# Two-layer perceiver on one core: the turned context rows of the second cross attention kept in DRAM and loaded, with deeper buffers, all norms of the samples at once, and a unit's exponential one step later

## The chip, the cores and the metric

The kernel runs on one core of one Trainium2 chip. The metric is the time of one execution on the device in microseconds (us), as the median of several runs. Besides the times there is one profiled execution of the kernel: a trace of every instruction on TensorE (PE, with its weight loads apart as PEld), VectorE (DVE), ScalarE (ACT), GpSimd (POOL) and SyncE (SP), of the DMA queues, and of the clock that TensorE was granted (1.00 is full speed).

## The reference

Sixteen samples `x` of 64 rows by 256 attend to sixteen contexts `ctx` of 1601 rows by 256. Two layers follow each other, all in float32. In each, a cross attention, a second mixing layer and a layer of experts are added to `x` in turn, each on the normalised `x`.

```
# layer 0, cross attention: 16 heads of 16, 5 sample points a head
K, V = ctx @ Wk.T + bk, ctx @ Wv.T + bv             # all 1601 rows
Qp = norm(x) @ Wq.T + bq;  off = Qp @ Woff.T + boff
ix = (position + off) mod length, scaled             # a real number per point
sk, sv = 0.5*((1-f)*K[floor(ix)] + f*K[floor(ix)+1]), the same with V
x += (softmax_over_5(Qp . sk / sqrt(16)) . sv) @ Wo.T + bo
# layer 0: sigmoid self attention, then 8 gelu experts, the best 2 of each row
# layer 1, cross attention: 16 heads of 64 over the same context
text, image = ctx[:, :77], ctx[:, 77:]               # 77 and 1524 rows
y  = softmax(q . (text Wk).T / 8) . (text Wv)
y += softmax(q . (image Wk_ip).T / 8) . (image Wv_ip)
x += y @ Wo.T + bo
# layer 1: state space scan over 64 rows, then 32 experts (best 4) and a shared one
```

The context is read twice: layer 0 projects all rows to keys and values, layer 1 uses the 77 text rows and the 1524 image rows of the same array.

## The kernel before

**Keys and values of layer 0.** `spans` (L237) cuts the 1601 rows of each sample into three stretches of 512 and a last one of 65. A stretch of 512 lies in a tile `cx` with four neighbouring rows on each of 128 partitions; `cx_load` (L240) loads it on SP's DMA queue, two stretches ahead, into two buffers. `keys_values` (L369) runs seven steps a sample: TensorE turns two rows a partition (four transposes of 128x128 at L153), ScalarE copies the result into `cxt` (L398), and TensorE multiplies the stretch before, already turned, by the joined key and value weights `wkv` (four banks of 128x512 in PSUM, L381 through L88). ScalarE copies each bank into the tile `kv` (L382, two buffers), and when a stretch is whole, ScalarE's DMA queue writes it to a table `tab` in DRAM (L385), one table for two samples.

**Sample points.** Beside these steps runs the generator `samples` (L300), four groups of two tiles of 128 rows. Each group normalises its rows (`normed`: VectorE's statistics and ScalarE's square root at L99), turns them, projects them to queries and offsets, and computes the indices `ix` and weights `wt` in some forty VectorE instructions. One step of it is issued with each step of the keys and values.

**Text rows.** From step 18 on the generator `texts` (L485) projects the 77 text rows of each sample to the keys and values of layer 1. Keys go to `ktd` in DRAM, kept sample by sample, in four stores for each four pairs of heads (L524); values go to `vtd`.

**Gathers and units.** From step 14 on, GpSimd gathers the sampled key and value rows out of the tables: `gather` (L416) issues ten indirect DMAs (L429), two of which halves make a unit of four heads for 128 rows; there are 32 units. `attend` (L436) works on a unit in two steps: the first forms the scores on VectorE and ends with the exponential on ScalarE (L459), the second normalises (L461 on) and weighs the values. `tick` (L1511) decides when: it is called between pieces of TensorE work with an estimate of their time in us, opens a new half unit every 16 of these us (12 in the cross attention), and takes the next step of a unit 42 after its gathers. `attended` counts finished units; it decides when the middle layers (self attention, experts) may use a tile and how long the plain cross steps run.

**Cross attention of layer 1.** The class `Cross` (L907) takes one sample and one pair of heads a step, 128 steps and three more to run out. The image rows of a sample lie in `cn` as they are in DRAM (`loads`, L915: eleven rows on each partition and 116 rows over, two buffers) with a column of ones added. For the scores they are needed turned: `turn` (L937) does that once a sample, 24 transposes on TensorE and ten copies, shared by VectorE (L84) and ScalarE, into `cT`, of which there is one buffer. It is called in the last step of the sample before (L1102), and for sample 0 in `begin` (L1175). A step (`step`, L1070) issues on TensorE: the scores of twelve blocks of 128 rows in three banks (L1087), the turn and the output of the step before the last (`turn_out`, L1061; `out`, L1020), the first third of the product of the step before with `cn` (`product`, L1059), the transposes that form the row maximum (L1109, L1119), the second third, the queries of the next step folded through the key weights (`fold`, L1015), the last third. VectorE takes the maxima straight from the banks (L1090), subtracts the maximum `mc` into `pt` (L1130), and ScalarE takes the exponentials there (L1131). The 116 rows over go by themselves (L1133, L1134), so there are four subtractions and four exponentials a step. In the middle of the step and at its end generators of other work are advanced by a step: first the rest of layer 0, then the state space (`Ssm`) and the router of layer 1.

**Order.** The instructions of TensorE, VectorE and ScalarE run in the order in which the program issues them (L1527). SP's and GpSimd's are ordered by the framework's scheduler, so a load is issued as soon as its buffer is free and those queued ahead of it are out. Each engine and each queue is in order: an instruction that waits holds what stands behind it.

**Memory on the chip.** `qbds` (queries in blocks) and `pts` (exponentials) are taken at the start from the pool `xw` (L217, L219) and zeroed by GpSimd (L1528 to L1531), though the cross attention alone uses them. The pool `kvp` of the keys and values is closed at the end of that stage, before `Cross` takes `cn` and `cT`.

Of the kernel before, what the change touches and what calls it, by code (L numbers as in the profile page):

```python
# [37 lines left out]
CM = IMG // P  # L38
CR = IMG - CM * P
NCH = CM + 1  # L40
NB = NCH // 4

# [23 lines left out]
def perceiver_kernel(ctx: ExitStack, tc: tile.TileContext, a: dict, out: bass.AP):  # L66
# [150 lines left out]
    qbds = [mk(xw, [P, NHP, 2, 2, S], f"qbd{i}") for i in range(2)]  # L217

    pts = [mk(xw, [P, NCH, P], f"pt{i}") for i in range(2)]  # L219
    tables = [mk(dram, [H0 * M, 4 * HD0], f"tab{j}") for j in range(NPAIR)]  # L220
    ktd = mk(dram, [B, P, NHP, TEXT], "ktd")
# [15 lines left out]
    spans = [(b, m0, RP if M - m0 >= RP * P else 1) for b in range(B) for m0 in range(0, M, RP * P)]  # L237
    cxs = {}

    def cx_load(i):  # L240
        if i < len(spans):
            b, m0, r = spans[i]
            w = min(P, M - m0)
            cx = cxs[i] = mk(kvp, [P, RP, D], "cx", bufs=2)
            nc.sync.dma_start(
                out=cx[:w, :r, :], in_=a["ctx"][b, m0 : m0 + w * r, :].rearrange("(p r) d -> p r d", r=r)
            )
# [3 lines left out]
    cx_load(1)  # L251
    nc.scalar.dma_start(out=x4, in_=a["x"].rearrange("(t p) d -> p t d", p=P))
# [46 lines left out]

    def samples(g):  # L300

        t0 = g * TG
        xn = normed(range(t0, t0 + TG), "s", sp)
        for _ in range(4 if g else 2):
            yield
        xt = turned(xn, TG, "s", sp)
        yield
# [9 lines left out]
        yield  # L317
# [3 lines left out]
        for t in range(TG):  # L321
# [13 lines left out]
            nc.vector.tensor_scalar(xs, xs, sgn[:, c], 1.0 / (M - 1), ALU.mult, ALU.mult)  # L335
        nc.vector.tensor_scalar(x_, x_, 2.0, -1.0, ALU.mult, ALU.add)
# [8 lines left out]
        nc.vector.tensor_tensor(x_, x_, f0, ALU.subtract)  # L345
        wg_ = wt[:, t0 : t0 + TG]
# [6 lines left out]
        for t in range(TG):  # L353
            j = t0 + t
            nc.vector.tensor_scalar(wt[:, j], wt[:, j], zl[:, j : j + 1], None, ALU.add)
            nc.vector.tensor_tensor(f0[:, t, :], f0[:, t, :], hbase, ALU.add)

# [9 lines left out]
        yield  # L367

    def keys_values():  # L369
# [3 lines left out]
        def project(i, cxt, q):  # L373
            nonlocal kv
            b, m0, r = spans[i]
            w = min(P, M - m0)
            if q == 0:
                kv = mk(kvp, [P, H0, RP, 2 * HD0], "kv", bufs=2)
# [11 lines left out]
        for i, (b, m0, r) in enumerate(spans):  # L390
            w = min(P, M - m0)
            cx = cxs.pop(i)
            cxt = mk(kvp, [P, RP, KC, P], "cxt")
            steps = (r + 1) // 2
            for q in range(steps):
# [4 lines left out]
                )  # L400
                if q + 1 == steps:
                    cx_load(i + 2)
# [33 lines left out]
    def attend(i):  # L436
# [21 lines left out]
        nc.vector.tensor_tensor(sc, sc, mx.unsqueeze(2).to_broadcast([P, HU, NK]), ALU.subtract)  # L458
        nc.scalar.activation(sc, sc, AF.Exp, scale=0.5 / math.sqrt(HD0))  # L459
# [1283 lines left out]
```

## Time and profile before

| | |
|---|---|
| median of 5 runs | 3315.1 us (3302.52 to 3331.89) |
| the profiled execution | 3343.09 us, span 3341.1 us |
| mean granted clock | 0.941 |
| TensorE busy | 2934.0 us, 88% of the span |
| VectorE, ScalarE, GpSimd busy | 1620.2, 1026.0, 819.1 us |
| moved by DMA | 326.06 MB, 97 GB/s over the span |

The span falls into stages that differ in what they wait for:

| from to (us) | work |
|---|---|
| 0 to 727 | keys and values of layer 0, sample points, text rows, first gathers, part of the middle layers |
| 727 to 942 | the rest of the middle layers, with gathers |
| 942 to 1400 | first steps of the cross attention, with the last gathers |
| 1400 to 1850 | cross attention beside the rest of layer 0 |
| 1850 to 3045 | cross attention beside the state space |
| 3045 to 3341 | the last experts |

In the profile a group such as "L88 PE MATMUL st<-qf,cT" is a line, an engine, an operation, the tile written and the tiles read; `st` and `mm` are banks of PSUM. A wait names the engine and the line that ended it; "remote" is a wait whose releaser the trace does not show. A share of DMA is the mean busy share of the core's 16 DMA engines. The chain of waits is followed back from the last instruction of the execution.

### The profile page before, as it was taken

To read this page: it belongs to the slowest core of one execution; us is meant where nothing else is said; L and a number is where in the kernel's file an instruction comes from. 1 tells how busy PE (TensorE), PEld (TensorE's weight loads), DVE (VectorE), ACT (ScalarE), POOL (GpSimd) and SP (SyncE) were. 2 spreads that over 40 slices of the span, in tenths; PEclk is the share of its full clock that TensorE was granted. 3 is DMA by queue.
4 is the path that set the end of the run, shared out by engine and by line. 5 is a ranking of instruction groups with operands and counts; after the bars stand their busy time and mean duration, and the time that the engine had idled before them with its cause. 6 is when DMAs were issued, how large, how long until landed. Compare 5 with 4: busy or idle time off the path is not lost.

```text
span 3341.1 us, 46546 instructions
## 1 busy us (share of the span) xinstructions
PE 2934.0 (88%) x17734; PEld 2405.1 (72%) x17734; DVE 1620.2 (48%) x4143; ACT 1026.0 (31%) x2379; POOL 819.1 (25%) x923
## 2 busy tenths in 40 slices
PE   8779877995668788888899899999999999999879
PEld 4444433564567777777798899989999999896667
DVE  2421113223345454555432567557754477655846
ACT  3223333432211221233243333334323343222421
POOL 0444334545535455300001001001100011000721
PEclk9889988997779898898999999999999999999999
DMA  6387754572421112111355212112210122003884
GB/s 201 101 142 153 244 154 110 166 205 80 126 63 31 45 42 60 44 49 34 101 174 167 61 55 65 49 43 69 68 34 30 43 73 65 29 1 105 254 244 123
DMA packets 339015, 326.06 MB, mean 98 GB/s; under 512 B 59349, under 2 KB 289017, under 8 KB 338281
## 3 DMA queue, kind: packets, MB, share of 16 engines
q1 hardware_dynamic: 186297, 225.11, 22.7%
q10 hardware_dynamic: 126928, 63.06, 6.8%
q0 software_dynamic: 25568, 34.91, 5.0%
q8 instruction: 141, 2.31, 0.3%
q14 instruction: 81, 0.66, 0.1%
HBM read 248.37 MB, written 74.62 MB: 97 GB/s over the span
## 4 chain that ended last, share of the span: by engine, by line
PE 75%; DVE 11%; another core or an unknown queue 5%; issue 3%; ACT 3%; DMA 3%; POOL 0%; SPq 0%; DVEq 0%; ACTq 0%; POOLq 0%
PE st L88 31%; PE mm L1059 19%; PE mm L88 16%; PE mm L153 5%; PE mm L1015 2%; DVE hs L1298 1%; PE mm L1045 1%; DVE mp L1090 1%; PE mm L984 1%; DMA wg<-in_guT 1%; DVE pt L1130 1%; PE mm L1109 1%; DVE hc L1303 0%; DMA yk<-y0d,sli 0%
## 5 line engine op out<-in xcount | busy, mean ns | idle before, releaser
L429 POOL DMA_INDIRECT g<-tab,ig x640 | 617.0, 964 | 751.4 <-DVE ig L427 548.8
L88 PE MATMUL st<-qf,cT 128*128 128x128 f32 x6144 | 761.8, 282 | 37.5 <-issue 19.9
L88 PEld LDWEIGHTS st<-qf,cT 128*128 128x128 f32 x6144 | 741.4, 199 | 46.1 <-issue 22.3
L1059 PE MATMUL mm<-cn,pt 128*128 128x257 f32 (+1 forms) x3072 | 757.0, 390 | 4.3 <-DVE cT L84 2.1
L1059 PEld LDWEIGHTS mm<-cn,pt 128*128 128x128 f32 (+1 forms) x3072 | 564.6, 193 | 92.1 <-issue 4.1
L88 PE MATMUL st<-wkv,cxt 128*128 128x512 f32 (+1 forms) x832 | 407.7, 637 | 54.0 <-ACT kv L382 34.6
L1090 DVE TENSOR_REDUCE mp<-st 128x128 f32<-128x512 f32 x384 | 261.1, 688 | 251.7 <-PE st L88 228.5
L88 PEld LDWEIGHTS st<-wkv,cxt 128*128 128x128 f32 (+1 forms) x832 | 159.7, 201 | 230.9 <-issue 174.6
L1130 DVE TENSOR_TENSOR pt<-st,mc 128x512 f32<-128x512 f32 (+1 forms) x384 | 224.2, 639 | 151.9 <-ACT mc L1121 141.4
L1131 ACT ACTIVATE pt<-pt 128x512 f32<-128x512 f32 (+1 forms) x384 | 207.1, 588 | 58.1 <-DVE pt L1130 53.2
L382 ACT COPY kv<-st 128x512 f32<-128x512 f32 (+1 forms) x208 | 119.4, 591 | 240.7 <-PE st L88 136.6
L1121 ACT COPY mc<-mm 128x128 f32<-128x128 f32 x128 | 33.9, 265 | 460.1 <-PE mm L1119 343.6
L1111 DVE TENSOR_REDUCE xmx<-mm 128x1 f32<-128x128 f32 x128 | 37.3, 292 | 231.2 <-PE mm L1109 180.4
L1068 ACT COPY ot<-mm 128x256 f32<-128x256 f32 x128 | 47.2, 369 | 300.0 <-PE mm L153 299.9
L920 POOL MEMSET cn<- 128x12 f32 x16 | 1.8, 120 | 549.5 <-PE mm L1059 519.1
L461 DVE TENSOR_REDUCE smx<-sc 128x4 f32<-128x20 f32 x32 | 5.4, 168 | 250.3 <-ACT sc L459 250.0
L1304 POOL TENSOR_TENSOR ys<-ys,hc 128x512 f32<-128x512 f32 x64 | 81.5, 1274 | 161.2 <-DVE hc L1303 160.9
L88 PE MATMUL mm<-xt,w 128*128 128x256 f32 (+1 forms) x512 | 102.8, 355 | 19.5 <-issue 11.6
L1388 POOL DMA_INDIRECT xb<-xnd,row x55 | 55.3, 1006 | 261.9 <-PE mm L1045 221.6
L88 PEld LDWEIGHTS mm<-xt,w 128*128 128x128 f32 x512 | 88.1, 214 | 37.7 <-issue 23.8
L1035 ACT COPY yt<-mm 128x64 f32<-128x64 f32 x128 | 27.1, 212 | 253.4 <-PE mm L88 219.9
L398 ACT COPY cxt<-mm 128x512 f32<-128x512 f32 (+1 forms) x112 | 60.8, 543 | 99.8 <-PE st L88 31.0
(455 smaller groups left out, 3986.9 us busy)
## 6 DMA issues: line engine op xcount, KB each, us to landing
tab<-kv ACTq DMA_DIRECT2D x48, 1024.0 KB
w<-in_gate SPq DMA_DIRECT2D x66, 512.0 KB
cx<-in_ctx SPq DMA_DIRECT2D x48, 512.0 KB
cn<-in_ctx SPq DMA_DIRECT2D x16, 1408.0 KB
wg<-in_guT SPq DMA_DIRECT2D x87, 256.0 KB
w<-in_lin SPq DMA_DIRECT2D x33, 512.0 KB
wk<-in_xwkiT SPq DMA_DIRECT2D x32, 512.0 KB
wd<-in_down1T SPq DMA_DIRECT2D x87, 128.0 KB
```

Source lines behind the costliest of these rows:

```text
L88: nc.tensor.matmul(o, lhsT=l, rhs=r, start=i == 0, stop=i == len(pairs) - 1)
L153: nc.tensor.transpose(t[:ncol, i, :rows], b, ident[:rows, :rows])
L382: nc.scalar.copy(kv[:w, :, c, :], pk[:w].rearrange("p (h e) -> p h e", h=H0))
L398: nc.scalar.copy(cxt[:, 2 * q : 2 * q + m, :, :w].rearrange("p r k n -> p (r k) n"), tp[:, : KC * m, :w])
L429: nc.gpsimd.indirect_dma_start(out=gf[:, (half * n + s) * 4 * HD0 : (half * n + s + 1) * 4 * HD0], out_offset=None, in_=tables[j], in_offs ...
L1015: nc.tensor.matmul(pf[:, k * P : (k + 1) * P], lhsT=w[:, hp % 4, k * P : (k + 1) * P], rhs=rhs, start=True, stop=True)
L1059: nc.tensor.matmul(po, lhsT=pt[:w, c, :], rhs=cn[:w, c, :], start=c == 0, stop=c == NCH - 1)
L1090: nc.vector.tensor_reduce(mp_[:, i, :], s.rearrange("p c n -> p n c"), AX.X, ALU.max)
L1130: nc.vector.tensor_tensor(o, st[i][:, :m, :], mc.to_broadcast([P, m, P]), ALU.subtract)
L1131: nc.scalar.activation(o, o, AF.Exp)
L1304: nc.gpsimd.tensor_tensor(y, y, hc, ALU.add)
L1388: nc.gpsimd.indirect_dma_start(out=x, out_offset=None, in_=xnd, in_offset=bass.IndirectOffsetOnAxis(ap=tb.row[:, i : i + 1], axis=0))
```

## The change

Image rows are cut as 512, 512 and 500, behind the 77 text rows, so that the stretches that layer 0 turns are those that the cross attention scores; what lies in `cxt` after a stretch is turned is stored to a new array `ctd` in DRAM, 512 KB a stretch, on SP's queue, and `turn` becomes three loads of 512 KB. The scores read these three tiles, `product` takes 128, 128 or 125 partitions a block, and three full subtractions and exponentials replace three and the one for the rest. The 125 wide stretch has its last three columns filled by two small copies (16 samples, two a sample). `turn(0)` moves from `begin` to just behind `loads(0)`, ahead of the middle layers.

More buffers ahead: `cx` three instead of two (a stretch is loaded three ahead), `cxt` three instead of two, `kv` four instead of two. To have the memory, `qbds` and `pts` are taken from a pool opened after the keys and values, and zeroed there (the zeroing of `pts` goes), and two tiles of the state space share the buffers of others.

The samples' rows are normalised and turned in one piece for all eight tiles; the groups take slices of it, and their work is spread over more steps. A unit takes three steps instead of two: a step ends ahead of the exponential, which is issued with the next. Text keys are stored for four samples side by side, one store instead of four.

```diff
-CM = IMG // P
-CR = IMG - CM * P
-NCH = CM + 1
-NB = NCH // 4
+SPAN = (P, P, 125)
+NB = len(SPAN)
+NCH = NB * RP
...
-    qbds = [mk(xw, [P, NHP, 2, 2, S], f"qbd{i}") for i in range(2)]
-
-    pts = [mk(xw, [P, NCH, P], f"pt{i}") for i in range(2)]
+    qbds = []
+
+    pts = []
...
-    ktd = mk(dram, [B, P, NHP, TEXT], "ktd")
+    ktd = mk(dram, [B // 4, P, NHP, 4 * TEXT], "ktd")
...
-    spans = [(b, m0, RP if M - m0 >= RP * P else 1) for b in range(B) for m0 in range(0, M, RP * P)]
+    spans = [(b, m0, w, r) for b in range(B) for m0, w, r in [(0, TEXT, 1)] + [(TEXT + s * RP * P, w, RP) for s, w in enumerate(SPAN)]]
+
+    ctd = mk(dram, [B, NB, P, RP * KC * P], "ctd")
...
-            cx = cxs[i] = mk(kvp, [P, RP, D], "cx", bufs=2)
+            cx = cxs[i] = mk(kvp, [P, RP, D], "cx", bufs=3)
...
     cx_load(1)
+    cx_load(2)
...
+    def turn_all():
+
+        xn = normed(range(NPAIR), "s", sp)
+        for _ in range(3):
+            yield
+        xts.append(turned(xn, NPAIR, "s", sp))
+        yield
+
+    xts = []
+
     def samples(g):
 
+
         t0 = g * TG
-        xn = normed(range(t0, t0 + TG), "s", sp)
-        for _ in range(4 if g else 2):
-            yield
-        xt = turned(xn, TG, "s", sp)
-        yield
+        xt = xts[0][:, :, g * TOK : (g + 1) * TOK]
+
+        def rest():
+            yield
+            if g:
+                yield
+
...
-        yield
+        yield from rest()
...
             if q == 0:
-                kv = mk(kvp, [P, H0, RP, 2 * HD0], "kv", bufs=2)
+                kv = mk(kvp, [P, H0, RP, 2 * HD0], "kv", bufs=4)
...
-            cxt = mk(kvp, [P, RP, KC, P], "cxt")
+            cxt = mk(kvp, [P, RP, KC, P], "cxt", bufs=3)
...
+                if r > 1 and w < P:
+
+                    nc.scalar.copy(
+                        cxt[:, 2 * q : 2 * q + m, :, w:].rearrange("p r k n -> p (r k) n"), tp[:, : KC * m, : P - w]
+                    )
                 if q + 1 == steps:
-                    cx_load(i + 2)
+                    cx_load(i + 3)
+                    if r > 1:
+                        nc.sync.dma_start(out=ctd[b, (m0 - TEXT) // (RP * P)], in_=cxt.rearrange("p r k n -> p (r k n)"))
...
         nc.vector.tensor_tensor(sc, sc, mx.unsqueeze(2).to_broadcast([P, HU, NK]), ALU.subtract)
+        yield
         nc.scalar.activation(sc, sc, AF.Exp, scale=0.5 / math.sqrt(HD0))
...
                 if hp % 4 == 3:
-                    for i in range(4):
-                        nc.sync.dma_start(out=ktd[q * 4 + i, :, hp - 3 : hp + 1, :], in_=kt[:, :, i * TEXT : (i + 1) * TEXT])
+                    nc.sync.dma_start(out=ktd[q, :, hp - 3 : hp + 1, :], in_=kt)
...
-            nc.sync.dma_start(
-                out=cn[:, :CM, :D], in_=a["ctx"][b, TEXT : TEXT + CM * P, :].rearrange("(p c) d -> p c d", c=CM)
-            )
-            nc.sync.dma_start(out=cn[:CR, CM, :D], in_=a["ctx"][b, TEXT + CM * P :, :])
+            m0 = TEXT
+            for i, w in enumerate(SPAN):
+                nc.sync.dma_start(
+                    out=cn[:w, i * RP : (i + 1) * RP, :D], in_=a["ctx"][b, m0 : m0 + w * RP, :].rearrange("(p r) d -> p r d", r=RP)
+                )
+                m0 += w * RP
...
-            self.kt[b] = load(self.xp, "kt", ktd[b], [P, NHP, TEXT], 1)
+            self.kt[b] = load(self.xp, "kt", ktd[b // 4, :, :, b % 4 * TEXT : (b % 4 + 1) * TEXT], [P, NHP, TEXT], 1)
...
-            cn = self.cn[b]
-            ct = self.ctx[b] = mk(self.xc, [P, KC, NCH * P], "cT", bufs=1)
-            i = 0
-            for k in range(KC):
-                d = slice(k * P, (k + 1) * P)
-                for c in range(0, CM, 4):
...
+            self.ctx[b] = [
+                load(self.xc, f"ct{i}", ctd[b, i].rearrange("p (r k n) -> p r k n", r=RP, k=KC), [P, RP, KC, P], 1) for i in range(NB)
+            ]
...
-                w = P if c < CM else CR
+                w = SPAN[c // RP]
...
-                        j = (i * 4 + c) * P
-                        mm(s[:, c, :], [(ct[:, k, j : j + P], qf[:, k, :]) for k in range(KC)])
+                        mm(s[:, c, :], [(ct[i][:, c, k, :], qf[:, k, :]) for k in range(KC)])
...
-                    c0 = i * 4
-                    m = 4 if i + 1 < NB else 3
-                    o = pt[:, c0 : c0 + m, :]
-                    nc.vector.tensor_tensor(o, st[i][:, :m, :], mc.to_broadcast([P, m, P]), ALU.subtract)
+                    o = pt[:, i * 4 : i * 4 + 4, :]
+                    nc.vector.tensor_tensor(o, st[i], mc.to_broadcast([P, 4, P]), ALU.subtract)
                     nc.scalar.activation(o, o, AF.Exp)
-                o = pt[:CR, CM, :]
-                nc.vector.tensor_tensor(o, st[-1][:CR, 3, :], mc[:CR, 0, :], ALU.subtract)
-                nc.scalar.activation(o, o, AF.Exp)
...
-            self.turn(0)
             self.loads(1)
...
-            dx = mk(mp, sh, "dx")
-            y = mk(mp, sh, "ys")
+            dx = mk(mp, sh, "mt")
+            y = mk(mp, sh, "mn")
...
     def attended():
-        return pace["sub"] // 2
+        return pace["sub"] // 3
...
-        for z in qbds:
-            nc.gpsimd.memset(z, 0.0)
-        for z in pts:
-            nc.gpsimd.memset(z[:, CM, :], 0.0)
...
-        early = chain([lengths()] + [samples(g) for g in range(NG)])
+        early = chain([lengths(), turn_all()] + [samples(g) for g in range(NG)])
...
+        xq = sx.enter_context(tc.tile_pool(name="xq", bufs=1))
+        for i in range(2):
+            qbds.append(mk(xq, [P, NHP, 2, 2, S], f"qbd{i}"))
+            nc.gpsimd.memset(qbds[i], 0.0)
+            pts.append(mk(xq, [P, NCH, P], f"pt{i}"))
         xc = sx.enter_context(tc.tile_pool(name="xc", bufs=1))
         cr = Cross(xc)
         cr.loads(0)
+        cr.turn(0)
```

More of the change, by code (lines that the diff above doesn't have):

```diff
@@ L241, in cx_load @@
         if i < len(spans):
-            b, m0, r = spans[i]
-            w = min(P, M - m0)
-            cx = cxs[i] = mk(kvp, [P, RP, D], "cx", bufs=2)
+            b, m0, w, r = spans[i]
+            cx = cxs[i] = mk(kvp, [P, RP, D], "cx", bufs=3)
             nc.sync.dma_start(
@@ L335, in samples @@
             nc.vector.tensor_scalar(xs, xs, sgn[:, c], 1.0 / (M - 1), ALU.mult, ALU.mult)
+            yield from rest()
         nc.vector.tensor_scalar(x_, x_, 2.0, -1.0, ALU.mult, ALU.add)
@@ L345, in samples @@
         nc.vector.tensor_tensor(x_, x_, f0, ALU.subtract)
+        yield from rest()
         wg_ = wt[:, t0 : t0 + TG]
@@ L356, in samples @@
             nc.vector.tensor_tensor(f0[:, t, :], f0[:, t, :], hbase, ALU.add)
+        yield from rest()
         nc.vector.tensor_scalar(ix[:, t0 : t0 + TG, :], f0, float(2 * HD0), None, ALU.mult)
@@ L366, in samples @@
             nc.vector.tensor_reduce(qb[:, t0 + t, :], y.rearrange("p (h d) -> p h d", d=HD0), AX.X, ALU.add)
-        yield
+        yield from rest()
     def keys_values():
@@ L374, in project @@
             nonlocal kv
-            b, m0, r = spans[i]
-            w = min(P, M - m0)
+            b, m0, w, r = spans[i]
             if q == 0:
-                kv = mk(kvp, [P, H0, RP, 2 * HD0], "kv", bufs=2)
+                kv = mk(kvp, [P, H0, RP, 2 * HD0], "kv", bufs=4)
             for c in range(2 * q, min(2 * q + 2, r)):
@@ L388, in project @@
                 )
-        for i, (b, m0, r) in enumerate(spans):
-            w = min(P, M - m0)
+        for i, (b, m0, w, r) in enumerate(spans):
             cx = cxs.pop(i)
-            cxt = mk(kvp, [P, RP, KC, P], "cxt")
+            cxt = mk(kvp, [P, RP, KC, P], "cxt", bufs=3)
             steps = (r + 1) // 2
@@ L940, in turn @@
                 return
-            cn = self.cn[b]
-            ct = self.ctx[b] = mk(self.xc, [P, KC, NCH * P], "cT", bufs=1)
-            i = 0
-            for k in range(KC):
-                d = slice(k * P, (k + 1) * P)
-                for c in range(0, CM, 4):
-                    n = min(4, CM - c)
-                    blocks = [cn[:, c + i_, d] for i_ in range(n)]
-                    tp = transposes(blocks)
-                    copy(i % 3, ct[:, k, c * P : (c + n) * P].rearrange("p (i n) -> p i n", n=P), tp[:, :n, :])
-                    i += 1
-                tp = transposes([cn[:CR, CM, d]])
-                nc.scalar.copy(ct[:, k, CM * P : IMG], tp[:, 0, :CR])
-                nc.scalar.copy(ct[:, k, IMG:], ct[:, k, : NCH * P - IMG])
+            self.ctx[b] = [
+                load(self.xc, f"ct{i}", ctd[b, i].rearrange("p (r k n) -> p r k n", r=RP, k=KC), [P, RP, KC, P], 1) for i in range(NB)
+            ]
         def queries(self, t, part):
```

## The prediction

> **What bounds the kernel now.** I read the page first: the engines' totals and the chain that ended last.
>
> ```profile
> PE 2934.0 (88%) x17734; PEld 2405.1 (72%) x17734; DVE 1620.2 (48%) x4143; ACT 1026.0 (31%) x2379; POOL 819.1 (25%) x923
> ...
> PE 75%; DVE 11%; another core or an unknown queue 5%; issue 3%; ACT 3%; DMA 3%; POOL 0%; SPq 0%; DVEq 0%; ACTq 0%; POOLq 0%
> ```
>
> TensorE carries three quarters of the chain, so a TensorE instruction that goes is worth its own time, unless TensorE was waiting there. Where it waits is read from the busy time by stage (columns: stretch, length, busy time and count of each engine, granted clock, DMA share, GB/s):
>
> ```profile
> 0.00:727.00 727.00, 609.05 (x1920) 330.21 (x1921) 183.52 (x603) 243.58 (x469) 293.24 (x318) 0.92 0.63 160
> 727.00:942.00 215.00, 132.48 (x627) 109.37 (x626) 75.17 (x234) 55.52 (x112) 97.35 (x103) 0.77 0.44 128
> 942.00:1400.00 458.00, 364.89 (x2412) 326.19 (x2411) 227.11 (x574) 87.91 (x240) 233.31 (x242) 0.90 0.17 40
> 1400.00:1850.00 450.00, 391.94 (x2720) 356.10 (x2717) 199.85 (x588) 145.88 (x328) 27.74 (x41) 0.94 0.34 104
> 1850.00:3045.00 1195.00, 1185.74 (x8801) 1087.72 (x8800) 745.20 (x1672) 408.84 (x996) 67.83 (x108) 1.00 0.16 47
> ```
>
> From 1850 us the cross attention is TensorE alone: busy 1185.7 of 1195 us at clock 1.00. Before 1400 us it idles: 118 us in keys and values, 83 in the middle layers, 93 in the first cross steps. Those are the stages in which GpSimd gathers (its busy column). The timeline of keys and values shows what such idle time looks like:
>
> ```profile
> 216.89 7.08 PE L88 MATMUL st<-wkv,cxt 128*128 128x512 f32 x16
> ...
> 228.32 0.58 ACT L382 COPY kv<-st 128x512 f32<-128x512 f32 x1 [4.01 <-remote]
> ...
> 238.62 0.94 POOL L429 DMA_INDIRECT g<-tab,ig  x1 [0.30 <-issue]
> ...
> 243.18 0.58 ACT L382 COPY kv<-st 128x512 f32<-128x512 f32 x1 [3.64 <-remote]
> ```
>
> All 16 matmuls are on record by 224 us, yet ScalarE gets the four banks at 228, 232, 239 and 243. The four copies fill one `kv` tile, so a late table write could explain the first wait alone. I read it as TensorE itself running late while a burst of gathers is out: such waits with no named releaser appear in every stage up to 1385 us, the last gather is issued at 1382, and none comes later. I call these the unnamed waits; they are 13.1% of the first stage's chain, 95 us.
>
> **The turn in the cross attention (-54).** At each of 16 samples 24 transposes, 10 copies and the waits around them go. Sample 1's turn in the timeline:
>
> ```profile
> 1070.73 1.52 PE L153 MATMUL mm<-ident,cn 128*128 128x128 f32 x12
> ...
> 1074.06 2.01 PE L1059 MATMUL mm<-cn,pt 128*128 128x257 f32 x8
> ```
>
> From 1070.73 to 1074.06 are 3.3 us on TensorE's own queue: 16 x 3.3 = 53, plus about 1 us for later waits on the copies. The other way of reading it agrees: between one L1111 and the next lie 12.3 us in a bare step, 16.5 in the ordinary step that turns; some 1 to 1.5 of the 4.2 are the text scores and their turn, which stay. Ends: 16 x 2.7 = 43 and 16 x 4.2 = 67.
>
> **The loads that take its place (0).** Three loads of 512 KB a sample on SP's queue, each waiting for the last score matmuls that read its third of the turned rows. One step's scores, and the next step's:
>
> ```profile
> 2051.10 3.73 PE L88 MATMUL st<-qf,cT 128*128 128x128 f32 x32
> ...
> 2054.89 1.95 PE L88 MATMUL st<-qf,cT 128*128 128x128 f32 x16
> ...
> 2063.43 2.84 PE L88 MATMUL st<-qf,cT 128*128 128x128 f32 x24
> ```
>
> A third is free about 1.9 us after its scores began and wanted 12.3 us after, so each load has some 10.4 us. What covers it is the step's own remainder (output, the three parts of the product, fold). What a load takes: the first context load, also 512 KB, is issued at 0.82 us and used at 4.79, so 4.0 us; the slowest row is
>
> ```profile
> 916.44 1.05 SPq L158 DMA_DIRECT2D wq<-in_xwq  x2
> ...
> 923.40 6.34 PE L88 MATMUL mm<-qt,wq 128*128 128x128 f32 x32 [5.64 <-DMA wq<-in_xwq]
> ```
>
> 7.0 us, the last of five loads together (2.2 MB in 8.2 us, 268 GB/s; the three new ones are 1.57 MB, 5.9 us). So 3 to 6 us of slack, cost 0; if the cover goes, each further us costs 15 (one per boundary). Behind these loads on SP wait weights, the state-space rows, the next natural rows; all are asked for a step or more early. The natural rows become three loads instead of two, same bytes: 0. The first sample's loads lie ahead of the expert weights at about 731 us, in a latency-bound stage: 1.57 MB at 268 GB/s is 5.9 us, part of it hidden: +4, ends 0 and +6.
>
> **The turned rows' stores (0).** 48 stores of 512 KB, SP's queue, behind the context load of three spans later and waiting for ScalarE's copy; the next context load waits behind each, but is now three spans early. 25.2 MB: 1700-1800 us moved 192 GB/s at a DMA share of 0.61, so 315 GB/s at full share, and 80 us of all engines. Against it, the text keys leave in 8 stores instead of 32, in runs of 4,928 bytes instead of 308: in 200-300 us SP's queue took 51.9% of the engines for 14,322 packets, 58 ns each, so 16,384 packets were 59 us and become 16. Net +37 us on a share of 0.63 over 727 us, so 0.68: not the bound. 32 more small ScalarE copies (L955 takes 0.21 us, so 7 us) lie on an engine busy 34% of the stage. A `cxt` buffer now also waits for its store before it is written again, but that is three spans on, some 6.5 us a step and six steps. The price on the key side: each load of text keys becomes 1,024 runs of 308 bytes, 3.7 us at 58 ns on 16 engines, asked for five steps before use: 0.
> [...]
>
> **Deeper buffers and the samples (-30).** The waits of the first stage, ScalarE's and TensorE's (total, times, longest):
>
> ```profile
> ACT kv L382 <- remote: 57.7, 16, 7.8
> ...
> ACT sd L99 <- DVE sd L98: 37.3, 4, 12.6
> ...
> ACT kv L382 <- DMA tab<-kv: 11.2, 3, 6.3
> ...
> PE mm L153 <- DVE xn L103: 9.2, 1, 9.2
> ```
>
> Norms at once turn four waits of ScalarE on the vector engine's sample work into one; behind the longest (12.6) TensorE stood 6.3 us for a `kv` copy. With the 9.2 above and 5.2 on L311 about 20 go; one wait of some 5 for eight norms together comes back: -15. Twice the `kv` buffers take the 11.2 on table writes: -10. Lighter text keys where the DMA share was 0.90: -5. The unnamed waits stay. The samples' later steps cost nothing: group 0's indices are ready in step 13, the gathers open in step 14. Ends: all 95 us of them go too, -125; the added traffic costs its net 37 us, +37. I take -30, the sum of the named rows.
> [...]
>
> **Exponentials one step later (-3).** ScalarE no longer stands at its exponential until the vector engine has the scores: 62.7 us over 14 waits. But two units are attended after the last gather, and their steps hardly notice; from L1111 to L1111
>
> ```profile
> 1414.62 0.29 DVE L1111 TENSOR_REDUCE xmx<-mm 128x1 f32<-128x128 f32 x1 [1.69 <-PE mm L1109]
> ...
> 1427.06 0.29 DVE L1111 TENSOR_REDUCE xmx<-mm 128x1 f32<-128x128 f32 x1 [1.36 <-PE mm L1109]
> ```
>
> 12.4 us with 4.5 us of that wait inside, against 12.3 (the next is 13.2). Behind it stands the `ot` copy, for which TensorE waited 7.2 us in all of 942-1400: -3, ends 0 and -20. Counted from the code, with three steps a unit instead of two all units still end in the same 27th cross step. Zeroing `qbd` moves behind the keys (3.5 us of GpSimd, which there already waits for the same memory at L920): 0. One exponential and one subtraction fewer a step are off TensorE's queue: 0.
>
> **Sum.** -54 + 0 + 4 + 0 - 30 - 3 = -83 on the profiled execution's 3343.1 us, 3260. That execution is 28 us above the median 3315.1; against the median: 3232.
>
> **Rivals.**
> - *Unnamed waits go with the buffers:* -83 - 95 = -178, 3137; if half, 3185. For it: they stand at `kv` copies. Against it: they are as dense at 942-1400, where the DMA share is 0.17 and nothing waits on tables.
> - *Buffers and samples bring nothing,* TensorE being late anyway: -53, 3262.
> - *The loads land late (the other sign).* SP is in order, and it does stand:
>
> ```profile
> SPq L1246 <- DVE db L1296: 176.9, 18, 17.2
> ```
>
> 9.8 us on average at a state-space load, which could be queued ahead of the turned rows. Past 10.4 us, every us costs 15, and a clock that has dropped adds about 1.8 a boundary (32 score matmuls took 5.46 us after a wait at 1044, 3.73 undisturbed). From landing 14.1 us after release on, 15 x (3.7 + 1.8) = 83 eats the gain; at 16.5 us it is +36, 3351. Against it: those waits end with vector work of the same step, before the scores.
> - *Stores crowd the first stage:* their 80 us land on the path, and the -30 is lost: 3315 - 53 + 80 = 3342.
>
> **How the numbers follow.** Forecast 0.42, own range 3200 to 3265; unnamed waits go 0.15; nothing from the buffers 0.20; late loads 0.11; crowded stores 0.06; the rest 0.06, near no change. 0.5% (17 us) is about what a measurement of this kernel can tell from no change. Faster: 0.42 + 0.15 + 0.20 = 0.77; slower 0.11 + 0.03 of the stores' case; same the remaining 0.09. The range leaves out the lower half of the first rival and the worst of the slower ones: 3155 to 3325.
>
> **What would show it.** Right: no L153 on `cn`; steps into a new sample at some 13.5 us; no TensorE wait on the `ct` loads; about 700 us for keys and values; unnamed waits still there until the last gather. Wrong: TensorE waiting for `ct` at the first scores of a sample, a half clock after it, or a first stage whose length moves by far more than 30 us either way.

## The result and the profile after

The changed kernel takes 3339.05 us (median of 28 runs, 3321.39 to 3355.2) against 3322.66 for the kernel before (54 runs): a ratio of 1.0054, 95% interval 1.0039 to 1.0068. It is slower by half a per cent. The forecast was 3232, in a range of 3155 to 3325, so both the sign and the range were missed.

The page of the changed kernel, engines and chain:

```profile
PE 2875.6 (86%) x17350; PEld 2351.9 (70%) x17350; DVE 1573.1 (47%) x3945; ACT 996.4 (30%) x2183; POOL 814.5 (24%) x921
...
PE 68%; DVE 11%; issue 5%; another core or an unknown queue 4%; DMA 4%; ACTq 3%; ACT 3%; SPq 1%; POOL 0%; DVEq 0%; POOLq 0%
PE st L87 29%; PE mm L1071 18%; PE mm L87 14%; ACTq L401 3%; PE mm L152 3%; PE mm L1027 2%; DMA wg<-in_guT 1%; DVE mp L1101 1%; PE mm L1057 1%; DVE hs L1303 1%; DVE pt L1139 1%; PE mm L1120 1%; PE mm L996 1%; ACT kv L398 1%
```

TensorE is busy 58 us less, as intended: the turn's instructions are gone. But a name is in the chain that was not there before: ACTq L401, 3%, some 107 us (3.2% of 3344.4). ACTq is ScalarE's own queue for DMA issues, and L401 is the write of `kv` to the table, the line L385 of before.

Busy time by stage of the changed kernel, cut where its own stages end (columns as in the prediction):

```profile
0.00:777.00 777.00, 606.67 (x1916) 330.95 (x1917) 179.31 (x590) 243.35 (x497) 284.96 (x313) 0.89 0.61 182
777.00:1004.00 227.00, 132.57 (x654) 109.23 (x653) 80.66 (x250) 54.24 (x106) 105.47 (x111) 0.78 0.46 131
1004.00:1435.00 431.00, 344.23 (x2302) 304.59 (x2302) 214.34 (x526) 83.52 (x198) 228.96 (x239) 0.92 0.20 53
1435.00:3033.00 1598.00, 1529.91 (x11152) 1401.91 (x11151) 906.77 (x2098) 527.81 (x1140) 95.65 (x149) 0.98 0.25 76
```

Cut by the same events (end of the last copy into `kv`, row maxima of cross steps 0, 24 and 127), before and after stand like this, each from one profiled execution; the last column is an experiment described below:

| stage | before | after | split (e13_split_all) |
|---|---|---|---|
| keys and values | 725 | 774 | 706 |
| middle layers | 226 | 230 | 223 |
| cross steps 0 to 23, with gathers | 451 | 431 | 431 |
| cross steps 24 to 127 | 1629 | 1598 | 1597 |
| last experts | 310 | 311 | 312 |

The profiled execution of before is 20 us above its median, that of the changed kernel 7 above, that of the split kernel at its median, so some 13 to 20 us of the differences from the column of before belong to that execution. Two more profiles of the changed kernel have 765 and 779 us for keys and values, 226 and 219 for the middle layers.

The cross attention gives 51 us, near the 57 forecast for the turn and the exponential together. Keys and values, forecast 30 us shorter, are 49 longer, with about the same busy time of TensorE (607 us to 777, against 610 to 728 before). The engines stand more.

ScalarE's timeline of the changed kernel shows where. The first write is that of the 125-partition stretch, the second that of the 77 text rows behind it (start, duration):

```profile
585.22 0.28 ACTq L401 DMA_DIRECT2D tab<-kv  x1
...
588.24 8.81 ACTq L401 DMA_DIRECT2D tab<-kv  x1
597.08 1.28 ACT L754 ACT_TABLE_LOAD   x1 [8.87 <-issue]
```

The issue of the small write holds ScalarE 8.81 us, and whatever is queued on ScalarE with it: the next instruction starts after 8.87 us of standing. (An ordinary wait holds what stands behind it in the same way: in the kernel before, ScalarE stood 12.60 us for `sd` until 97.30 us, the copies behind it came only then, and TensorE waited 6.26 us for one of them.) In the kernel before, the place of the 8.81 us reads

```profile
586.80 0.37 ACTq L385 DMA_DIRECT2D tab<-kv  x1
...
589.87 0.33 ACTq L385 DMA_DIRECT2D tab<-kv  x1
```

All issues of table writes together are 24.3 us before and 141.3 after; 122.9 of that are 15 long ones, every one of them the 77-row write behind a 125-partition write (the 16th of the narrow writes has none behind it). They began 1.5 to 11 us after the narrow write's issue, but in 13 of the 15 cases they ended 8.9 to 12.5 us after it, and in two 18.

The packets of the queue (q10, the one that carries ScalarE's writes) show the write itself. First the narrow write above from 589 to 597 us, then the full write of before from 588 to 591; the last number is the time of the packets as a share of 16 engines:

```profile
q10 hardware_dynamic: 1460, 0.75, 31.7%
```

```profile
q10 hardware_dynamic: 1771, 0.91, 104.5%
```

So the narrow write keeps about 5 engines' worth of packets under way (16 x 0.317 = 5.1), the full one all 16. The packets of the 16 narrow writes take 10.3 to 19.4 us from first to last, with 3.0 to 5.8 under way in the mean of each write; those of the 48 full writes of before take 3.9 us in the median, with 15 under way. All 15 long issues end 2.2 to 4.3 us before the last packet of the narrow write ahead of them. So it is the narrow write that they wait for, though not until it is wholly out.

### The profile page after: what moved, and what is told of

The parts are those of the page before. It is cut to its first block, busy times and chain, and to the rows that moved or that the text cites. A ratio compares the mean times of both kernels' runs of the same rounds, so it can differ in the third digit from the quotient of the medians.

```text
span 3344.4 us, 45642 instructions
## 1 busy us (share of the span) xinstructions
PE 2875.6 (86%) x17350; PEld 2351.9 (70%) x17350; DVE 1573.1 (47%) x3945; ACT 996.4 (30%) x2183; POOL 814.5 (24%) x921
## 4 chain that ended last, share of the span: by engine, by line
PE 68%; DVE 11%; issue 5%; another core or an unknown queue 4%; DMA 4%; ACTq 3%; ACT 3%; SPq 1%; POOL 0%; DVEq 0%; POOLq 0%
PE st L87 29%; PE mm L1071 18%; PE mm L87 14%; ACTq L401 3%; PE mm L152 3%; PE mm L1027 2%; DMA wg<-in_guT 1%; DVE mp L1101 1%; PE mm L1057 1%; DVE hs L1303 1%; DVE pt L1139 1%; PE mm L1120 1%; PE mm L996 1%; ACT kv L398 1%
## 5 line engine op out<-in xcount | busy, mean ns | idle before, releaser
L87 PE MATMUL st<-qf,ct 128*128 128x128 f32 x6144 | 756.6, 280 | 33.7 <-issue 28.7
L87 PEld LDWEIGHTS st<-qf,ct 128*128 128x128 f32 x6144 | 731.9, 196 | 44.4 <-issue 35.0
L87 PE MATMUL st<-wkv,cxt 128*128 128x512 f32 (+2 forms) x832 | 398.9, 626 | 61.3 <-ACT cxt L413 35.0
L1139 DVE TENSOR_TENSOR pt<-st,mc 128x512 f32<-128x512 f32 x384 | 241.3, 684 | 170.9 <-ACT mc L1132 135.9
L87 PEld LDWEIGHTS st<-wkv,cxt 128*128 128x128 f32 (+2 forms) x832 | 157.3, 198 | 232.2 <-issue 186.3
L1140 ACT ACTIVATE pt<-pt 128x512 f32<-128x512 f32 x384 | 228.9, 628 | 51.1 <-DVE pt L1139 47.7
L398 ACT COPY kv<-st 128x512 f32<-128x512 f32 (+2 forms) x208 | 120.3, 590 | 251.7 <-PE st L87 133.3
L1122 DVE TENSOR_REDUCE xmx<-mm 128x1 f32<-128x128 f32 x128 | 37.3, 292 | 183.6 <-PE mm L1120 176.0
L87 PE MATMUL mm<-xt,w 128*128 128x256 f32 (+1 forms) x512 | 99.6, 348 | 25.0 <-DMA w<-in_gate 13.6
L1309 POOL TENSOR_TENSOR mn<-mn,hc 128x512 f32<-128x512 f32 x64 | 81.5, 1274 | 160.8 <-DVE hc L1308 156.4
L413 ACT COPY cxt<-mm 128x512 f32<-128x512 f32 (+2 forms) x112 | 60.6, 546 | 125.6 <-PE mm L152 55.8
```

Of the source, the lines that this page charges most:

```text
L87: nc.tensor.matmul(o, lhsT=l, rhs=r, start=i == 0, stop=i == len(pairs) - 1)
L398: nc.scalar.copy(kv[:w, :, c, :], pk[:w].rearrange("p (h e) -> p h e", h=H0))
L413: nc.scalar.copy(cxt[:, 2 * q : 2 * q + m, :, :w].rearrange("p r k n -> p (r k) n"), tp[:, : KC * m, :w])
L1139: nc.vector.tensor_tensor(o, st[i], mc.to_broadcast([P, 4, P]), ALU.subtract)
L1140: nc.scalar.activation(o, o, AF.Exp)
L1309: nc.gpsimd.tensor_tensor(y, y, hc, ALU.add)
```

## Experiments

**Chips.** The experiments ran in five groups, which I call jobs, each on one chip with the kernel before beside it. The five chips are of two kinds. On three of them the kernel before took 3314 to 3321 us; on two, 3063 and 3069. I call them the slow and the quick chips; as no chip appears in two jobs, it is not shown that the difference stays with the chip. The measurement above and the profile of before are of the slow kind. Ratios are compared within a job or between chips of one kind.

Three theories were set up for ScalarE's standing. *Narrow:* a transfer of 125 partitions is spread over few DMA engines (above, 3.0 to 5.8 engines' worth of packets under way), drains slowly (10.3 us or more), and the next issue waits for it. *Crowding:* the stores of the turned rows slow all writes. *Depth:* with four `kv` buffers ScalarE runs ahead until its queue is full.

### The narrow transfers split

The edit, shown at the table write; e1_split_all does the same at the loads of `cx` and `cn`, e2_split_tab at the table write alone:

```diff
+    def pieces(w):
+        return ((0, 112), (112, w)) if w == 125 else ((0, w),)
...
-                nc.scalar.dma_start(
-                    out=tab[b % 2, :, m0 : m0 + w * r, :].rearrange("h (p r) e -> p h (r e)", r=r),
-                    in_=kv[:w, :, :r, :].rearrange("p h r e -> p h (r e)"),
-                )
+                for p0, p1 in pieces(w):
+                    nc.scalar.dma_start(
+                        out=tab[b % 2, :, m0 + p0 * r : m0 + p1 * r, :].rearrange("h (p r) e -> p h (r e)", r=r),
+                        in_=kv[p0:p1, :, :r, :].rearrange("p h r e -> p h (r e)"),
+                    )
```

> The changed kernel, with every transfer of the 125-partition stretch (table write, context load, natural rows) cut in two, 112 and 13 partitions; the bytes are the same. In the changed kernel ScalarE stands 141 us at the issue of its table writes, against 24 before, nearly all of it at the 77-row write that follows the 125-partition write. Narrow theory (a write of 125 partitions is spread over few DMA engines, is slow, and the next write cannot be handed over until it has drained): the issue time falls from 141 to about 30 us, keys and values end at 700 to 735 instead of 777, time 3260 to 3295. Crowding theory (the 25 MB of stores of turned rows slow all writes): nothing changes, 3339 within 10. Depth theory (four buffers let ScalarE run ahead until the queue is full): nothing changes, since as many bytes are outstanding.

> The changed kernel with only the table write of the 125-partition stretch cut in 112 and 13 partitions; context loads and natural rows as in the changed kernel. Narrow theory, with ScalarE's standing as the whole price: the same time as with all three cut, within 8 us (3260 to 3300). If the narrow loads cost too, some 10 to 30 us more than with all three cut. Crowding and depth theories: 3339 within 10.

Measured on a slow chip: 3272.4 us, ratio to before 0.9846 (0.9807 to 0.9886) with all three split, and 3284.6, 0.9887 (0.9841 to 0.9933), with the table write alone. The issues of table writes fall from 141 to 54 and 67 us (not to the 30 expected), and the last copy into `kv` comes at 704 and 715 us instead of 774. The two are not told apart; the table write alone is at least most of it. The same place in the split kernel (e13_split_all, a repeat):

```profile
531.93 1.99 ACTq L406 DMA_DIRECT2D tab<-kv  x2
...
536.02 0.30 ACTq L406 DMA_DIRECT2D tab<-kv  x1
```

Two pieces are issued in 1.99 us and the 77-row write behind them takes 0.30. Not all standing is gone: the two pieces together take 1.6 to 3.0 us to issue, once 8.5, and all issues of table writes together 56 us against 24 before. Narrow holds; crowding and depth, which both said no change, fall as explanations of the 62 us.

The split was run twice more beside the unchanged changed kernel:

> The changed kernel as it is, again, beside the kernel before on the same chip. The job with the turn back on TensorE ran on a chip on which the kernel before takes 3063 us and no wait without a releaser is in the chain; the other job's chip took 3320. Here the ratio to before is what is asked for: about 1.005 on a chip like the slow one. On a chip like the quick one the narrow theory gives a ratio above that of e1_split_all by 0.015 to 0.03, since ScalarE's standing at its issue does not hang on the chip.

> e1_split_all again, as the base for the runs beside it. On a chip like the slow one 0.985 of before, as measured; on one like the quick one 0.972 to 0.985, since there e4_turn_te took 0.990 and the turn is worth 30 to 60 us.

> The changed kernel again. On the slow chip 1.005 of before, as twice measured. On the quick chip, by the narrow theory: 1.5 to 3% above e13_split_all, 3025 to 3090 us; if the slow chip's waits are what makes the narrow write dear: within 15 us of e13_split_all.

> e1_split_all again, the base for the others here. Slow chip: 3265 to 3285. Quick chip: 2980 to 3000, that is 35 to 55 us below e4_turn_te's 3033, by the forecast's term for the turn.

Both jobs fell on slow chips. Changed kernel 3338.3 and 3334.2 (ratios 1.0051 and 1.0066), split 3277.1 and 3272.0 (0.9874 and 0.9871): the narrow transfers cost 61 and 62 us. What they cost on a quick chip was not measured.

### The kernel before with one narrow write

```diff
+                for p0, p1 in (((0, 125), (125, P)) if m0 == 2 * RP * P else ((0, w),)):
...
-                    out=tab[b % 2, :, m0 : m0 + w * r, :].rearrange("h (p r) e -> p h (r e)", r=r),
+                        out=tab[b % 2, :, m0 + p0 * r : m0 + p1 * r, :].rearrange("h (p r) e -> p h (r e)", r=r),
```

> The kernel before, with the table write of the third 512-row stretch of each sample cut in 125 and 3 partitions; nothing else changes, so no stores of turned rows and two kv buffers. Narrow theory: this alone makes the kernel slower by 30 to 90 us (3350 to 3410), with ScalarE standing at table writes, since the 125-partition part is spread over few engines. Crowding and depth theories: no change but one more issue a sample, 16 x 0.4 = 6 us at most: 3315 to 3330.

Measured on the slow chip of the first job: 3406.2 us, ratio 1.0255 (1.0215 to 1.0295). One write of each sample cut in 125 and 3 partitions costs the kernel before 86 us, with no store of turned rows and two `kv` buffers. All issues of table writes are 185 us. The longest stand in its ScalarE timeline is this, both pieces together:

```profile
417.60 18.27 ACTq L386 DMA_DIRECT2D tab<-kv  x2
435.91 0.59 ACT L399 COPY cxt<-mm 128x512 f32<-128x512 f32 x1 [18.34 <-issue]
```

Of the width of a write the traces show this: packets worth 5.1 engines are under way with 125 partitions, worth some 16 with 128 (the two rows of q10 above). That cutting 125 into 112 and 13 takes most of the wait away (issues of table writes 141 us before the split, 54 with it), and that cutting 128 into 125 and 3 makes it (24 and 185), is shown by the runs; why so few are under way with 125 is not.

### Two buffers instead of four for `kv`

```diff
-                kv = mk(kvp, [P, H0, RP, 2 * HD0], "kv", bufs=4)
+                kv = mk(kvp, [P, H0, RP, 2 * HD0], "kv", bufs=2)
```

> The changed kernel with two kv buffers instead of four, as before. Depth theory: the time at the issue of table writes falls from 141 us to some 30, keys and values end near 735, time about 3300. Narrow theory: ScalarE or TensorE stands at the copy into kv instead of at the issue, keys and values end at 777 or later, time 3335 to 3370. Crowding theory: as the narrow theory.

Measured: 3340.6 us, ratio 1.0064 (1.0037 to 1.0091), no different from the changed kernel, with 126 us still at the issues and the last copy into `kv` at 765. Of its waits (total, times, longest) the first is ScalarE's standing at its issues, seen at the copy behind them; the second, on a table write's landing, comes back beside it:

```profile
ACT cxt L413 <- issue: 50.7, 13, 13.8
...
ACT kv L398 <- DMA tab<-kv: 30.6, 11, 8.0
```

Depth falls: two buffers neither free the queue nor cost anything more. The slow write holds ScalarE either way.

### The turn and the stores

e4_turn_te is the split kernel with the context rows turned on TensorE again; the stores stay. In e5_turn_te_no_stores the stores and the small copies go too; the last two lines of the edit are its alone.

```diff
-            self.ctx[b] = [
-                load(self.xc, f"ct{i}", ctd[b, i].rearrange("p (r k n) -> p r k n", r=RP, k=KC), [P, RP, KC, P], 1) for i in range(NB)
-            ]
+            cn = self.cn[b]
+            ct = self.ctx[b] = [mk(self.xc, [P, RP, KC, P], f"ct{i}", bufs=1) for i in range(NB)]
+            for i, w in enumerate(SPAN):
+                for q in range(2):
+                    tp = transposes([cn[:w, i * RP + 2 * q + t, k * P : (k + 1) * P] for t in range(2) for k in range(KC)])
+                    copy(2 * i + q, ct[i][:, 2 * q : 2 * q + 2, :, :w].rearrange("p r k n -> p (r k) n"), tp[:, :, :w])
...
-                    if r > 1:
-                        nc.sync.dma_start(out=ctd[b, (m0 - TEXT) // (RP * P)], in_=cxt.rearrange("p r k n -> p (r k n)"))
```

> The kernel with the split transfers (e1_split_all, 3272 us), but the context rows are turned on TensorE again, once a sample, 24 transposes and their copies into the three tiles; the stores of the turned rows stay, the loads go. By the forecast's term for the turn (54, ends 43 and 67) less the 4 us of the first loads: 3310 to 3340. If the loads only move the time elsewhere: less than 25 us above 3272. Steps that turn 16 to 17 us from one row maximum to the next instead of 13.6.

> As e4_turn_te, and the 48 stores of turned rows and the 32 small copies that fill the last three columns go too, so that keys and values have the same traffic as before but the new cut, deeper buffers and the samples at once. Forecast's term (stores cost nothing): the same time as e4_turn_te within 10 us. Crowding (the stores' 25 MB lie on the path of keys and values): 25 to 80 us faster than e4_turn_te, and keys and values end that much earlier.

> The kernel of e4_turn_te again. On the slow chip, where e1_split_all took 3272, 3277 and 3272: by the forecast's term 3310 to 3340. On the quick chip 3033 again.

All three fell on quick chips: 3033.2 us (ratio 0.9903, 0.9886 to 0.9920) with the turn on TensorE, 3039.6 (0.9926, 0.9910 to 0.9943) without the stores as well, and 3040.3 (0.9909) in the repeat. Taking 25 MB of stores away makes nothing faster: crowding falls, on a quick chip; on a slow one it was not tried. Of the split kernel with loads there is no run on a quick chip but one that also moves the table writes (next experiment); it took 2987.0 beside e4_turn_te, 46 us less, in a job where no other base stood.

The steps show the turn's price directly. From row maximum to row maximum across a sample's boundary, the changed kernel:

```profile
1942.21 0.29 DVE L1122 TENSOR_REDUCE xmx<-mm 128x1 f32<-128x128 f32 x1 [1.69 <-PE mm L1120]
1955.83 0.29 DVE L1122 TENSOR_REDUCE xmx<-mm 128x1 f32<-128x128 f32 x1 [1.69 <-PE mm L1120]
```

That is 13.6 us, against 16.5 at the same boundary before (1909.99 to 1926.49). Over the ten boundaries beside the state space the mean falls from 17.04 to 13.98, by 3.1; 16 of these are 49 us. The turn put back takes 16.2 to 17.4 again.

The step behind this boundary is the first to score the new sample, with the rows just loaded. On TensorE it begins like this:

```profile
1959.67 0.60 PE L152 MATMUL mm<-ident,pet 128*77 128x128 f32 x4
1960.11 3.74 PE L87 MATMUL st<-qf,ct 128*128 128x128 f32 x32
```

The scores follow without a gap and take as long as an undisturbed step's (3.73 us), the step takes 12.8 us in both kernels, and no wait of TensorE in the whole profile names a load of `ct`.

### Table writes on SP's queue

```diff
-                    nc.scalar.dma_start(
+                    nc.sync.dma_start(
                         out=tab[b % 2, :, m0 + p0 * r : m0 + p1 * r, :].rearrange("h (p r) e -> p h (r e)", r=r),
```

> e1_split_all with the table writes issued on SP's queue instead of ScalarE's. If ScalarE's standing at its own issues (61 us of the execution, 18 of them of 1.5 us or more) still holds keys and values: 10 to 30 us faster than 3272. If the table writes hold the context loads and stores that stand behind them on SP instead: 0 to 40 us slower.

> The table writes on SP's queue, again (2987 us on the quick chip, with no base beside it). If ScalarE's issues still hold keys and values: 10 to 30 us below e13_split_all. If not: within 8 us of it.

On a quick chip 2987.0 us, ratio 0.9755 (0.9739 to 0.9772); on a slow one 3266.9, 0.9855 (0.9786 to 0.9925), beside 3272.0 for the split kernel. The last copy into `kv` comes 12 us earlier (693 against 705), the end 5: by these two runs not told from nothing. So what is left of ScalarE's standing at its issues in the split kernel is not shown to cost anything. On the slow chips this version and the split kernel beat both kernels of the case.

### Samples and buffers put back

e6_samples_by_group is the split kernel with norms, turns and steps of the samples by group, as before; e8_buffers_back is the split kernel with two buffers each, and the context loads two stretches ahead. The edit of e8:

```diff
-            cx = cxs[i] = mk(kvp, [P, RP, D], "cx", bufs=3)
+            cx = cxs[i] = mk(kvp, [P, RP, D], "cx", bufs=2)
...
-    cx_load(2)
...
-                kv = mk(kvp, [P, H0, RP, 2 * HD0], "kv", bufs=4)
+                kv = mk(kvp, [P, H0, RP, 2 * HD0], "kv", bufs=2)
...
-            cxt = mk(kvp, [P, RP, KC, P], "cxt", bufs=3)
+            cxt = mk(kvp, [P, RP, KC, P], "cxt", bufs=2)
...
-                    cx_load(i + 3)
+                    cx_load(i + 2)
```

> e1_split_all with the samples' norms, turns and steps by group as before. Forecast's term: 15 us slower than e12_split_all_again on the slow chip. If the unnamed waits cover it: within 8 us.

> e1_split_all with two buffers each of cx, cxt and kv, context loads two stretches ahead. Forecast's term: 10 us slower than e12_split_all_again for the waits on table writes. If a cxt buffer must also wait for its store and the next context load is late behind it: 20 to 60 us slower.

On a slow chip 3269.5 us (ratio 0.9854, 0.9811 to 0.9897) and 3277.6 (0.9864, 0.9814 to 0.9915), beside 3277.1 for the split kernel. Putting the samples back is 8 us faster, the buffers 0.5 slower, both within the interval of some 14 us: neither brings on a slow chip what was forecast. Both at once were not undone. The stages of e6 say more: with the samples by group, keys and values take 724 us, 14 to 19 longer than in the profiles of the three runs of the split kernel, and the middle layers 212, 11 to 13 shorter. So the 15 us forecast for the samples may well be there in their stage and be given back in the next; it is one execution of e6, and why is not shown.

### Without the gathers

```diff
-            nc.gpsimd.indirect_dma_start(
-                out=gf[:, (half * n + s) * 4 * HD0 : (half * n + s + 1) * 4 * HD0],
...
-            )
+            nc.gpsimd.memset(gf[:, (half * n + s) * 4 * HD0 : (half * n + s + 1) * 4 * HD0], 0.5)
```

> e1_split_all without the gathers: GpSimd fills the tiles of sampled rows with a constant, in as many instructions, so the sampled rows of layer 0 are left out; everything after them is done as ever. If the waits without a named releaser come with the gathers: they go from the chain (6% of 3279 us in e1_split_all, 190 us), keys and values end at 590 to 660 instead of 704, the cross steps that had gathers beside them take 12.3 to 14 us instead of 18, time 3020 to 3120. If they come from the other traffic, the loads and stores: they stay, and the time falls by less than 60 us, to 3210 or more.

> e1_split_all with the gathers left out (their tiles are filled with a constant), again. On the quick chip this took 2986 us and e9_tab_on_sp, with all gathers, 2987. On the slow chip: if the unnamed waits come with the gathers, 3030 to 3130 and less than 1% of such waits in the chain; if the slow chip has them whatever the kernel does, 3230 or more and still 4% or more of them.

On a quick chip (e10, one run) 2986.5 us, where e9_tab_on_sp with all its gathers took 2987.0; the two differ in the queue of the table writes as well, which was worth 5 us on a slow chip. On a slow chip (e15) 2991.7, where e13_split_all beside it took 3272.0: 280 us less, below the lower end of what was expected. Chain and stages of e15_no_gathers on the slow chip:

```profile
PE 81%; DVE 10%; DMA 4%; ACT 3%; issue 1%; SPq 0%; ACTq 0%; DVEq 0%; POOLq 0%
```

```profile
0.00:588.00 588.00, 564.23 (x1914) 312.65 (x1915) 177.13 (x589) 245.77 (x496) 33.80 (x355) 1.00 0.73 224
588.00:780.00 192.00, 138.17 (x724) 117.84 (x724) 88.25 (x272) 57.55 (x112) 14.49 (x124) 0.83 0.43 136
780.00:1106.00 326.00, 323.30 (x2419) 297.10 (x2418) 219.98 (x544) 88.62 (x208) 16.60 (x183) 1.00 0.18 52
```

There is no unnamed wait left, TensorE is busy 323 of 326 us in the first cross steps, and the clock there is 1.00 instead of the 0.91 of e13_split_all. On the slow chips the unnamed waits come with the gathers; in the profiles of quick chips none is listed, with gathers (e9_tab_on_sp, e16_turn_te) or without (e10_no_gathers).

What of the gathers makes them was to be told by plain loads in their place:

```diff
-            nc.gpsimd.indirect_dma_start(
...
+            nc.sync.dma_start(
+                out=gf[:, (half * n + s) * 4 * HD0 : (half * n + s + 1) * 4 * HD0],
+                in_=tables[j][s * P : (s + 1) * P, :],
+            )
```

> e1_split_all with each gather replaced by a plain load of as many bytes from the same table, 128 fixed rows, issued on SP's queue; the choice of rows by index is left out. On the slow chip: if the traffic of the gathers makes the unnamed waits, 3200 or more, with 4% or more of such waits in the chain; if it is that they are indirect and issued by GpSimd, 2985 to 3060 and less than 1% of such waits. On the quick chip: 2980 to 3040 either way.

The job fell on a quick chip: 3041.4 us. That is 54 above e9_tab_on_sp on another quick chip, with DMA at 6% of the chain instead of 4, and tells nothing of the slow chips, where the question stays open.

## Why the prediction was wrong

- **The turn, -54: right.** 49 us by the steps (ten of them, taken for 16), inside 43 to 67; the cross attention as a whole gave 51.
- **The loads in its place, 0: right. The first ones, +4: not told.** The scores of a new sample follow without a gap, and TensorE waits for no load of `ct`. The middle layers took 219 to 230 us in three profiles of the changed kernel and 226 in that of before, so 4 us could not be seen. The rival of late loads did not come.
- **The stores, 0: not contradicted.** Without them the kernel was no faster, on a quick chip. The rival "stores crowd the first stage" gave 3342, close to the 3339 measured, but by a cause that the split excludes: the split kernel still makes every store and is 62 us faster.
- **The new cut, no term: this is the step that failed.** The prediction counted the bytes of the new stretches and their packets, and wrote "same bytes: 0" for the natural rows; it never asked what a stretch of 125 partitions does to its transfers. The table write of that stretch has no term at all. In place of nothing stand 61 and 62 us, and on the kernel before 86. One of the prediction's own signs of being wrong came: a first stage that moves by more than 30 us, here 49 longer.
- **Deeper buffers and the samples, -30: wrong on the slow chips.** The named waits did go. Before, ScalarE waited 37.3 us for the samples' norms and 11.2 for table writes; the waits of the changed kernel in its first stage (0 to 778 us) read

```profile
ACT kv L398 <- remote: 63.8, 16, 9.9
...
ACT sd L98 <- DVE bst L94: 3.5, 1, 3.5
```

  and no copy into `kv` waits for a table write. The time did not follow: undone, the two parts cost 0.5 us and nothing. The unnamed waits, 57.7 us at the same copies before, are still there with 63.8 (44 and 51 in two profiles of the split kernel), and what the named waits took would lie beside them. That reading is argued, not shown; what speaks for it is the quick chips, which have no such waits: there everything but the turn, with the transfers split, is worth 28 and 30 us (e16_turn_te, e4_turn_te), near the 33 forecast for buffers, samples and exponential.
- **The exponential, -3: not tested by itself.**
- **The unnamed waits: the reading held, the size did not.** They were read as TensorE running late while gathers are out, and forecast to stay with deeper buffers. They stay, and they go with the gathers; that it is TensorE that runs late no run shows. But they were taken for 95 us of one stage; without gathers 280 us go, 120 of them in keys and values (706 to 586, by the last copy into `kv`) and 118 in cross steps 0 to 23 (431 to 313).

The sum corrected by these terms: -54 + 4 - 3 + 62 and 0 for buffers and samples make +9, or +14 with the 49 us that the turn measured, against +16 for the kernel; the +4 and the -3 in it are the forecast's own, unmeasured.

## What to carry to other kernels

A cut of the data is also a cut of its transfers: before a tile's partition count is changed, look at every DMA that carries it. Here a count of 125 was dear (61 and 62 us, in the kernel before 86), and two pieces of 112 and 13 were cheap (54 us at the issues instead of 141); other counts were not tried for a write of this size. The price appeared as time at the issue of the next DMA on the same queue (122.9 of 141.3 us), and as that queue was ScalarE's, it held ScalarE's computation (8.87 us in the row shown). And a named wait need not be worth its time where another wait may end at the same moment (the deeper buffers, forecast at 10 us for the waits on table writes, cost 0.5 us when undone): with a wait that the profile cannot name beside it, count it as nothing at the low end.

## What the runs showed of the hardware

- A table write of 1,000 KB from 125 partitions kept 3.0 to 5.8 engines' worth of packets under way and took 10.3 us or more from first packet to last, where one of 1,024 KB from 128 partitions in the kernel before kept 15 and took 3.9 us in the median. It held the next issue on its queue until 8.9 to 12.5 us after its own, in two cases 18. Written from 112 and 13 partitions, the two pieces together took 1.6 to 3.0 us to issue, once 8.5, and the write behind them 0.3 to 0.6 (e13_split_all).
- The chips are of two kinds for this kernel: 3314 to 3321 and 3063 to 3069 us for the kernel before. The difference goes with the gathers: 640 indirect DMAs cost 280 us on a slow chip (3272.0 against 2991.7), and on a quick one 0.5 us lie between two kernels that differ in one more point (2987.0 and 2986.5). Yet the gathers' own rows are alike; e13_split_all on a slow chip, then e9_tab_on_sp on a quick one:

```profile
L456 POOL DMA_INDIRECT g<-tab,ig x640 | 613.1, 958 | 727.8 <-DVE ig L454 430.5 <-issue 174.0 <-DVE x__604 L347 79.2
```

```profile
L456 POOL DMA_INDIRECT g<-tab,ig x640 | 611.8, 956 | 456.8 <-DVE ig L454 172.9 <-issue 169.5 <-DVE u__605 L349 78.6
```

  Each takes 958 and 956 ns, in all 613 and 612 us. What differs is the waits, GpSimd's own before the gathers among them (728 and 457 us), and the mean granted clock (0.944 and 0.973). What makes a chip slow is open.
